# Sorting the routed experts of a two-loop mixture: one sort for the first loop of one group and the second loop of the group ahead of it

## The chip, the cores and the metric

The kernel runs on one NeuronCore of one Trainium2 chip. The metric is device time in microseconds of one execution; a kernel's time is the median of its runs. Lower is better.

## The reference, cut to what matters

A batch of 16 sequences, each 512 tokens by 128 features, goes through four pre-normed residual layers. The last one is what the change is about: a mixture of 8 experts, run twice (two "loops") with the same weights, each token going to its two best experts.

```python
x = x + attn0(layernorm(x))          # 16 heads of 8, no mask
x = x + ffn0(layernorm(x))           # silu-gated, hidden 384
x = x + attn1(layernorm(x))          # 16 heads of 8, q and k normed, causal
x = x + moe(layernorm(x))

def moe(z):
    for _ in range(2):                               # LOOPS
        z_norm = rmsnorm(z, norm_w)
        scores = softmax(z_norm @ router_w)          # 8 experts
        topk_vals, topk_idx = top_k(scores, 2)
        topk_vals = topk_vals / (sum(topk_vals) + EPS)
        mixed = 0
        for e in range(8):
            mixed = mixed + cw[:, e:e+1] * swiglu(z_norm, w1[e], w3[e], w2[e])   # 128 -> 256 -> 128
        z = z + mixed
    return z
```

The second loop of a token depends on nothing but its own first loop, so loops of different sequences may be mixed freely.

## The kernel before

The program is unrolled and every engine's order is fixed by hand. The outer driver is a loop over *slots* (the `while slot < last ...` loop at the end of the kernel), each cut into 7 parts. A sequence takes 32 slots (`PERIOD`) of the first attention (names `s_a`, `e_a`, `mx_a`), starting at slot 32b for sequence b, and 32 slots of the causal second attention (`s_c`, `e_c`, `masked_c`), starting at slot 32b + 73. Each slot issues two exponentials of either stream that is alive; so the n-th `e_a` or `e_c` row of a trace tells which slot it belongs to, and slots can be laid on the time axis. Normally both streams run side by side; from slot 529 on only the causal one is left, and it ends at slot 594.

Between these fixed passes stand *tasks*, generators that are stepped where their pace asks for it: `front(b)` (layer norm, projections, feed-forward), `middle(b)` (the same for the second attention, then `close()`, which finishes the attention layer, writes `zkeep[b]` and `nkeep[b]` to DRAM and routes the sequence for its first loop). `route()` computes the router's logits and writes the one-hot choices (`chosen`) and weights (`cw`) of a sequence; in a trace its matmuls are `pl_m` when `close()` calls it and `pl_r` when the second loop does. The last two sequences (14 and 15) are not sorted: `all_experts` runs every expert on every token (`gg_u`, `gu_u`, `py_u`).

The other 14 sequences form groups, `GROUPS = (3, 3, 3, 3, 2)`. A group is queued (`running`) when its last sequence has been routed, and `experts(grp)` is then the single `active` task. For each of the two loops it does, in order:

- `dispatch`: a counting sort in some twenty small VectorE instructions and two matmuls into `pc`, which gives each (token, choice) a row in a DRAM buffer where every expert's rows are padded to whole tiles of 128. It ends with `owner`, an integer expert number for each tile. Then, for each sequence, one SP load of `znl` from `nkeep` (one buffer) and 8 indirect GpSimd DMAs, the *sends* (`sent<-znl,places`);
- `tiles`: for each tile of 128 rows, in fours: `rows` loaded from `sent` (which waits for all the sends), transposed (`pr`, `rT`), two gate/up and two down passes (`gu`, `h`, `py`, `y`) with that expert's 384 KB of weights, loaded ahead by SP into four buffers `w`; SP reads the expert number from `owner` first (`value_load`). `y` goes back to DRAM (`back<-y`);
- the *gathers*: for each sequence, 8 indirect GpSimd DMAs (`got<-back,places`), and 8 VectorE multiply-adds into `z`. After the first loop the sequence is normed again and routed into the same group; after the second, `xold` is added and the output written.

A sort over n sequences has a fixed number of tiles, `TOP_K * 4 * n + E - 1` = 8n + 7, whatever the data: 31 for n = 3, 23 for n = 2. `pace()` sets how many steps of the active task a slot takes, so that a group is done when the next one is due; no more than two steps go into each of four parts, so 8 a slot. GpSimd and SP keep one order for everything that they do: GpSimd also adds residuals (`x`, `z`), works on the second attention's queries (`both_c`) and raises variances to -0.5 (`rs_*`, `ss_*`).

Of the kernel before, what the change touches and what calls it, by code (L numbers as in the profile page):

```python
# [44 lines left out]
GROUPS = (3, 3, 3, 3, 2)  # L45
# [26 lines left out]
def kernel(  # L72
# [78 lines left out]
    MAXB = max(GROUPS) * NT  # L151
# [235 lines left out]
    groups, x2s = {}, {}  # L387
# [230 lines left out]
    def middle(b):  # L618
# [65 lines left out]
        def close():  # L684
            yield 0
            x2 = x2s.pop(b)
            pool.tensor_tensor(x2, x2, bo_r.unsqueeze(1).to_broadcast([P, NT, D]), ALU.add)
            yield 0
            oT = yield from feature_major(o(), f"o{b}", tag="xT_om", bufs=1)
            po = bank(f"ao_{b}")  # L690
            for k in range(NT):
                pe.matmul(
                    po[:, k * P : (k + 1) * P], oT[:, k * P : (k + 1) * P], w1T[:, 3 * D : 4 * D],
                    start=True, stop=True,
                )
            x3 = xs.tile([P, NT, D], F32, tag="x3", name=f"x3_{b}", bufs=1)
            dve.tensor_tensor(
                x3.rearrange("p t d -> p (t d)"), po, x2.rearrange("p t d -> p (t d)"), ALU.add
            )
            nc.sync.dma_start(xkeep[b], x3)  # L700
            yield 0

            if b >= B - ALL:
                z, mv, rs = yield from layernorm(x3, f"m{b}", tag="qmT_a")
                ss = small.tile([P, NT], F32, tag="ss", name=f"ss_m{b}")
                pool.tensor_tensor(ss, rs, rs, ALU.mult)
                pool.tensor_tensor(ss, ss, mv[:, :, 1], ALU.mult)
                yield 0
                yield from all_experts(b, z, ss)
                return  # L710
            i = next(i for i in range(len(GROUPS)) if b < sum(GROUPS[: i + 1]))
            if i not in groups:
                groups[i] = Group(i)
            z, mv, rs = yield from layernorm(x3, f"m{b}", x3)
            nc.sync.dma_start(zkeep[b], z)
            ss = small.tile([P, NT], F32, tag="ss", name=f"ss_m{b}")
            pool.tensor_tensor(ss, rs, rs, ALU.mult)
            pool.tensor_tensor(ss, ss, mv[:, :, 1], ALU.mult)
            zn = yield from normed(z, ss, f"m{b}_0", z)
            nc.sync.dma_start(nkeep[b], zn)  # L720
            yield from route(zn, groups[i], b - groups[i].first, f"m{b}_0", tag="xT_om", bufs=1)
            if b == sum(GROUPS[: i + 1]) - 1:
                running.append(i)
# [12 lines left out]
    class Group:  # L736


        def __init__(self, i):
            self.i = i  # L740
            self.first = sum(GROUPS[:i])
            self.n = GROUPS[i]
            self.blocks = self.n * NT
            self.tiles = TOP_K * self.blocks + E - 1
            self.loop(0)

        def loop(self, k):
            name = f"{self.i}_{k}"
            nb = self.blocks
            self.chosen = small.tile([P, TOP_K, E, MAXB], F32, tag="chosen", name=f"chosen_{name}")[:, :, :, :nb]  # L750
            self.cw = small.tile([P, TOP_K, MAXB], F32, tag="cw", name=f"cw_{name}", bufs=4)[:, :, :nb]

# [155 lines left out]
    fetched = {loop: [] for loop in range(LOOPS)}  # L908

    def dispatch(grp, loop, dst, name):  # L910
# [34 lines left out]
        picked = small.tile([P, TOP_K, E, MAXB], F32, tag="picked", name=f"picked_{name}", bufs=1)[:, :, :, :nb]  # L945
        for i in range(TOP_K):
            dve.tensor_tensor(picked[:, i], grp.chosen[:, i], upto3, ALU.mult)
# [7 lines left out]
        ends = small.tile([1, MAXT, E], F32, tag="ends", name=f"ends_{name}", bufs=1)[:, :nt]  # L955
# [6 lines left out]
        owner = small.tile([1, MAXT], I32, tag="owner", name=f"owner_{name}")  # L962
        dve.tensor_scalar(owner[:, :nt], ef, float(E - 1), None, ALU.min)
# [3 lines left out]
        for k in range(grp.n):  # L967
            zn = work.tile([P, NT, D], F32, tag="znl", name=f"znl_{name}_{k}", bufs=1)
            nc.sync.dma_start(zn, nkeep[grp.first + k])
            yield FETCH  # L970
            for t in range(NT):
                for i in range(TOP_K):
# [9 lines left out]
                    for load in fetched[loop]:  # L982
                        after(ins, load)
                    grp.sends.append(ins)
                    yield 0
        fetched[loop] = []
        grp.places, grp.owner = places, owner

    def tiles(grp, src, dst, loads, name):

        batches = [(q, min(4, grp.tiles - q)) for q in range(0, grp.tiles, 4)]
# [11 lines left out]
        def fetch(i):  # L1003
            w = work.tile([P, WC], F32, tag="w", name=f"w_{name}_{i}", bufs=4)
            e = nc.sync.value_load(grp.owner[0:1, i : i + 1], min_val=0, max_val=E - 1)
            nc.sync.dma_start(w, wcat[bass.ds(e, 1), :, :].rearrange("e p c -> p (e c)"))
            ws[i] = w

        ws = {}
        for i in range(batches[0][1]):  # L1010
            fetch(i)
        rows = fetch_rows(*batches[0])
        yield FETCH
        for b, (q, n) in enumerate(batches):
# [5 lines left out]
            if b + 1 < len(batches):  # L1020
                rows = fetch_rows(*batches[b + 1])
# [38 lines left out]
    def experts(grp):  # L1060
        for loop in range(LOOPS):
            name = f"{grp.i}_{loop}"
            yield from dispatch(grp, loop, sent[loop], name)
            yield SEND
            yield from tiles(grp, sent[loop], back[loop], fetched[loop], name)
            yield SEND
            places, cw = grp.places, grp.cw
            if loop + 1 < LOOPS:
                grp.loop(loop + 1)
            for k in range(grp.n):  # L1070
                b = grp.first + k
                z = work.tile([P, NT, D], F32, tag="z", name=f"z_{name}_{k}")
                nc.sync.dma_start(z, zkeep[b])
                got = work.tile([P, NT, TOP_K, D], F32, tag="gath", name=f"got_{name}_{k}", bufs=1)
                for t in range(NT):
                    for i in range(TOP_K):
                        j = k * NT + t
                        pool.indirect_dma_start(
                            out=got[:, t, i, :], out_offset=None, in_=back[loop][: grp.tiles * P, :],
                            in_offset=bass.IndirectOffsetOnAxis(ap=places[:, i, j : j + 1], axis=0),  # L1080
                        )
                        yield 0
                yield FETCH
                for t in range(NT):
                    for i in range(TOP_K):
                        j = k * NT + t
                        dve.scalar_tensor_tensor(
                            z[:, t, :], got[:, t, i, :], cw[:, i, j : j + 1], z[:, t, :],
                            ALU.mult, ALU.add,
                        )  # L1090
                    yield 0
                if loop + 1 < LOOPS:
                    nc.sync.dma_start(zkeep[b], z)
                    ss = small.tile([P, NT], F32, tag="ss", name=f"ss_{name}_{k}")
                    sq = work.tile([P, D], F32, tag="y", name=f"zsq_{name}_{k}", bufs=1)
                    for t in range(NT):
                        act.activation(sq, z[:, t, :], AF.Square, accum_out=ss[:, t : t + 1])
                    yield 0
                    pool.tensor_scalar(ss, ss, 1.0 / D, None, ALU.mult)
                    zn = yield from normed(z, ss, f"{name}_{k}")  # L1100
                    nc.sync.dma_start(nkeep[b], zn)
                    yield from route(zn, grp, k, f"r{name}_{k}", tag="xT_r", bufs=1)
                else:
                    xold = work.tile([P, NT, D], F32, tag="znl", name=f"xold_{name}_{k}", bufs=1)
                    nc.sync.dma_start(xold, xkeep[b])
                    yield FETCH
                    pool.tensor_tensor(z, xold, z, ALU.add)
                    nc.sync.dma_start(out[b].rearrange("(t p) d -> p t d", p=P), z)

    def expert_steps(n):  # L1110
        batches = (TOP_K * n * NT + E + 2) // 4
        mixed = n * (TOP_K + 1) * NT
        return LOOPS * (6 + TOP_K * n * NT + 9 * batches + mixed) + 15 * n

    def expert_waits(n):
        return LOOPS * (2 * SEND + (2 * n + 1) * FETCH) + n * FETCH

    def pace(i, now):

        todo, waits = ([count(n) for n in GROUPS[i:]] for count in (expert_steps, expert_waits))  # L1120
        until = PERIOD * (B - 1) + BEHIND + PERIOD + LAG
        rate = sum(todo) / (until - now - sum(waits))
# [48 lines left out]
    while slot < last or tasks or active is not None or running:  # L1171
        slot += 1
        for part in range(NPARTS):
# [5 lines left out]
            if part in PARTS:  # L1179
# [9 lines left out]
                if active is None and running:  # L1189
                    i = running.pop(0)  # L1190
                    grp = groups.pop(i)
# [5 lines left out]
    assert not groups  # L1197
# [31 lines left out]
```

## Time and profile before

| | |
|---|---|
| time of three runs | 3253.62 us (median), 3214.41, 3256.63 |
| the profiled execution | 3232.08 us, its span 3230.4 us |
| mean granted TensorE clock | 0.832 |
| PE (matmul) busy | 2893.9 us, 90% |
| VectorE busy | 2205.2 us, 68% |
| ScalarE busy | 1753.2 us, 54% |
| GpSimd busy | 698.1 us, 22% |
| loads of an expert's weights (`w<-wcat`) | 294, 384 KB each, 4.1 us to landing |
| sends, gathers | 224 and 224, 977 and 976 ns each on GpSimd |
| all DMA | 254.28 MB, 79 GB/s |

Every recorded instruction goes through one helper, so the line number is L59 nearly everywhere and groups are told apart by their tiles. Busy PE is not PE at its peak: matmuls are pipelined and their ends modelled.

### The profile page before, as it was taken

The page shows a single profiled execution, that of the slowest core. Times are in us where ns is not written, and L with a number is a line of the kernel's source. Part 1 is how long each engine was busy: PE and PEld are TensorE (multiplying, and loading weights), DVE is VectorE, ACT ScalarE, POOL GpSimd, SP SyncE. Part 2 cuts the span into 40 slices and gives each one's busy share as a digit, 9 for nine tenths or more (in the row PEclk, how much of TensorE's full clock was granted, in tenths as well). Part 3 has the DMA queues.
Part 4 walks back from the last instruction along what each step waited for, and adds up shares of the span by engine and source line. Part 5 has one row for each costly group of instructions (what it writes and reads, how often), then busy time and mean ns, then how long its engine had stood idle before and what let it go on. Part 6 is the DMA issues. An engine that isn't in the chain of part 4 may idle for free. (4 is left out here: it accounts for less than half of the span.)

```text
span 3230.4 us, 55826 instructions
## 1 busy us (share of the span) xinstructions
PE 2893.9 (90%) x19302; PEld 1732.5 (54%) x19302; DVE 2205.2 (68%) x6700; ACT 1753.2 (54%) x3867; POOL 698.1 (22%) x834
## 2 busy tenths in 40 slices
PE   6999999999998998999989899989989887788978
PEld 3444545455754565565456456446546546465555
DVE  5767677777676768667777866777776664646556
ACT  4656666575654656565566656566655643333322
POOL 1010001003022313303221421330240331412220
PEclk7978878797966998796799889589979859679889
DMA  3000000002411341241133233114224225343441
GB/s 111 4 4 1 8 14 8 14 11 79 137 54 42 109 129 56 87 150 49 50 112 105 77 104 118 43 59 142 83 75 147 90 67 162 97 148 94 131 126 53
DMA packets 192283, 254.28 MB, mean 79 GB/s; under 512 B 18945, under 2 KB 124673, under 8 KB 192001
## 3 DMA queue, kind: packets, MB, share of 16 engines
q1 hardware_dynamic: 176656, 221.16, 22.2%
q0 software_dynamic: 14336, 29.39, 3.2%
q8 instruction: 154, 2.52, 0.3%
q14 instruction: 129, 1.05, 0.1%
q10 hardware_dynamic: 1008, 0.15, 0.0%
HBM read 189.55 MB, written 64.23 MB: 79 GB/s over the span
## 5 line engine op out<-in xcount | busy, mean ns | idle before, releaser
L59 DVE CUSTOM_DVE_ANT_0 masked_c<-s_c,mask 128x128 f32<-128x128 f32 (+3 forms) x1024 | 501.2, 489 | 482.9 <-PE s_c L59 405.0
L59 DVE TENSOR_REDUCE mx_a<-s_a 128x1 f32<-128x512 f32 x1024 | 656.3, 683 | 190.2 <-PE s_a L59 186.9
L59 ACT ACTIVATE e_a<-s_a 128x512 f32<-128x512 f32 x1024 | 556.4, 597 | 245.9 <-PE s_a L59 240.1
L59 ACT ACTIVATE e_c<-s_c 128x512 f32<-128x512 f32 (+3 forms) x1024 | 392.3, 436 | 490.9 <-PE s_c L59 489.6
L59 PE MATMUL s_a<-qkT_a 32*128 32x512 f32 x2048 | 423.5, 576 | 21.6 <-DVE mx_c L59 4.5
L59 PEld LDWEIGHTS s_c<-qkT_c 32*128 32x128 f32 x2048 | 155.8, 215 | 476.6 <-issue 175.9
L59 PE MATMUL s_c<-qkT_c 32*128 32x128 f32 (+3 forms) x2048 | 335.8, 481 | 19.7 <-DVE x L59 6.9
L59 PE MATMUL gu<-rT,w 128*128 128x128 f32 x2352 | 314.5, 284 | 41.4 <-ACT rT L59 18.0
L59 PE MATMUL acc_a<-e_a,vpad 128*32 128x512 f32 x2048 | 351.0, 764 | 0.0
L59 PEld LDWEIGHTS gu<-rT,w 128*128 128x128 f32 x2352 | 285.4, 195 | 73.7 <-ACT rT L59 33.2
L59 POOL DMA_INDIRECT got<-back,places x224 | 218.6, 976 | 295.9 <-DMA back<-y 233.5
L59 PEld LDWEIGHTS s_a<-qkT_a 32*128 32x128 f32 x2048 | 185.9, 210 | 176.8 <-issue 33.3
L59 POOL DMA_INDIRECT sent<-znl,places x224 | 218.8, 977 | 243.7 <-DMA znl<-nkeep 85.2
L59 PE MATMUL s_a<-qmT_a,halves 32*128 32x512 f32 x1024 | 256.4, 494 | 0.0
L59 PE MATMUL acc_c<-e_c,vpad 128*32 128x512 f32 (+3 forms) x2048 | 236.0, 526 | 8.1 <-ACT e_c L59 8.1
L59 ACT ACTIVATE h<-gu 128x256 f32<-128x256 f32 x294 | 112.2, 384 | 170.1 <-PE gu L59 165.3
L59 PE MATMUL py<-w,h 128*128 128x128 f32 x1176 | 164.7, 283 | 9.1 <-DVE h L59 5.6
L59 DVE SCALAR_TENSOR_TENSOR h<-h,gu 128x256 f32<-128x256 f32 x294 | 121.8, 414 | 71.2 <-ACT h L59 70.0
L59 PE MATMUL s_c<-ident_b,mask 128*128 128x128 bf16 x1024 | 164.1, 249 | 0.0
L59 PEld LDWEIGHTS py<-w,h 128*128 128x128 f32 x1176 | 144.9, 192 | 26.8 <-DVE h L59 11.6
L59 PE MATMUL pm_c<-ident_r,mpad 128*128 128x128 f32 x256 | 89.2, 370 | 47.1 <-DVE mpad L59 43.3
L59 DVE TENSOR_TENSOR h<-h,gu 128x256 f32<-128x256 f32 x294 | 123.7, 421 | 10.1
(288 smaller groups left out, 4338.8 us busy)
## 6 DMA issues: line engine op xcount, KB each, us to landing
w<-wcat SPq DMA_DIRECT2D x294, 384.0 KB, 4.1
rows<-sent SPq DMA_DIRECT2D x66, 256.0 KB, 6.4
back<-y SPq DMA_DIRECT2D x66, 256.0 KB, 5.7
w_u<-wcat SPq DMA_DIRECT2D x32, 384.0 KB, 3.2
z<-zkeep SPq DMA_DIRECT2D x28, 256.0 KB, 2.7
znl<-nkeep SPq DMA_DIRECT2D x28, 256.0 KB, 3.0
x<-in_L_attn_x_dram SPq DMA_DIRECT2D x16, 256.0 KB, 3.0
xkeep<-x SPq DMA_DIRECT2D x16, 256.0 KB, 2.0
```

Of the source, the lines that this page charges most:

```text
L59: ins = method(*args, **kwargs)
```

## The change

`GROUPS` becomes seven groups of two. A `Batch` takes the place of a `Group` and holds rows (sequence, loop): batch i sorts the first loop of group i together with the second loop of group i - 1. So there are 8 batches: batch 0 has the first loops of two sequences, batches 1 to 6 have four rows each, batch 7 has the last two second loops. In place of 10 sorts with 8 x 31 + 2 x 23 = 294 tiles there are 8 with 6 x 39 + 2 x 23 = 280.

Batch i is queued as group i was, when its group's last sequence has been routed. Its gathers go first to the first-loop rows, which are normed and routed into batch i + 1 (created then or by the next `close()`, whichever comes first), then to the second-loop rows, which are written out. Batch 7 is queued by batch 6 at its end. The DRAM buffers `sent` and `back` alternate by batch, and grow from 31 to 39 tiles each, which are zeroed at the start.

Three small things go with it: the products of the sort are formed in place in `chosen` (the tile `picked` goes); `ends` takes the buffer of `y`; and `owner` is no longer one instruction in `dispatch` but one for every 16 tiles, made by VectorE just ahead of the weight load of tiles 0, 16 and 32.

```diff
-GROUPS = (3, 3, 3, 3, 2)
+GROUPS = (2, 2, 2, 2, 2, 2, 2)
+OWNERS = 16
...
-    MAXB = max(GROUPS) * NT
+    MAXB = max(a + b for a, b in zip((*GROUPS, 0), (0, *GROUPS))) * NT
...
-    class Group:
+    class Batch:
         def __init__(self, i):
             self.i = i
-            self.first = sum(GROUPS[:i])
-            self.n = GROUPS[i]
+            self.rows = [(b, 0) for b in members(i)] + [(b, 1) for b in members(i - 1)]
+            self.n = len(self.rows)
...
-        picked = small.tile([P, TOP_K, E, MAXB], F32, tag="picked", name=f"picked_{name}", bufs=1)[:, :, :, :nb]
+        picked = grp.chosen
         for i in range(TOP_K):
-            dve.tensor_tensor(picked[:, i], grp.chosen[:, i], upto3, ALU.mult)
+            dve.tensor_tensor(picked[:, i], picked[:, i], upto3, ALU.mult)
...
-        ends = small.tile([1, MAXT, E], F32, tag="ends", name=f"ends_{name}", bufs=1)[:, :nt]
+        ends = work.tile([1, MAXT, E], F32, tag="y", name=f"ends_{name}", bufs=1)[:, :nt]
...
-        owner = small.tile([1, MAXT], I32, tag="owner", name=f"owner_{name}")
-        dve.tensor_scalar(owner[:, :nt], ef, float(E - 1), None, ALU.min)
...
         def fetch(i):
             w = work.tile([P, WC], F32, tag="w", name=f"w_{name}_{i}", bufs=4)
-            e = nc.sync.value_load(grp.owner[0:1, i : i + 1], min_val=0, max_val=E - 1)
+            j = i % OWNERS
+            if j == 0:
+                owner = small.tile([1, OWNERS], I32, tag="owner", name=f"owner_{name}_{i}")
+                n = min(OWNERS, grp.tiles - i)
+                dve.tensor_scalar(owner[:, :n], grp.ends_before[:, i : i + n], float(E - 1), None, ALU.min)
+                owners[i // OWNERS] = owner
+            e = nc.sync.value_load(owners[i // OWNERS][0:1, j : j + 1], min_val=0, max_val=E - 1)
             nc.sync.dma_start(w, wcat[bass.ds(e, 1), :, :].rearrange("e p c -> p (e c)"))
...
     def experts(grp):
-        for loop in range(LOOPS):
-            name = f"{grp.i}_{loop}"
-            yield from dispatch(grp, loop, sent[loop], name)
-            yield SEND
-            yield from tiles(grp, sent[loop], back[loop], fetched[loop], name)
-            yield SEND
-            places, cw = grp.places, grp.cw
+        name, there, here = f"{grp.i}", sent[grp.i % 2], back[grp.i % 2]
+        loads = fetched[grp.i % 2]
+        yield from dispatch(grp, there, loads, name)
+        yield SEND
+        yield from tiles(grp, there, here, loads, name)
+        yield SEND
+        places, cw = grp.places, grp.cw
+        for k, (b, loop) in enumerate(grp.rows):
...
             if loop + 1 < LOOPS:
...
+                then = batch(grp.i + 1)
+                yield from route(zn, then, then.rows.index((b, loop + 1)), f"r{name}_{k}", tag="xT_r", bufs=1)
...
+        if grp.i + 1 == len(GROUPS):
+            running.append(grp.i + 1)
```

## The prediction

> **What bounds the kernel now.** I read the page's busy shares first, then the windows, then GpSimd's timeline and the waits of the last 600 us.
>
> ```profile
> PE 2893.9 (90%) x19302; PEld 1732.5 (54%) x19302; DVE 2205.2 (68%) x6700; ACT 1753.2 (54%) x3867; POOL 698.1 (22%) x834
> PEclk7978878797966998796799889589979859679889
> ```
>
> TensorE is the busiest engine, but 90% and a granted clock that swings between 0.5 and 1 say that a busy microsecond is no fixed amount of work. So I price by windows of 16 slots, cut where a slot's first exponential starts. Columns: start:end, length, busy time (instructions) of PE, PEld, DVE, ACT, POOL, clock, DMA share, GB/s.
>
> ```profile
> 507.70:582.10 74.40, 70.13 (x503) 39.30 (x500) 51.68 (x158) 51.40 (x111) 6.68 (x11) 0.91 0.04 12
> 582.10:651.10 69.00, 65.47 (x412) 32.85 (x404) 50.73 (x159) 40.72 (x86) 6.35 (x6) 0.70 0.03 9
> 651.10:724.20 73.10, 68.97 (x515) 39.54 (x512) 53.39 (x167) 51.82 (x113) 6.68 (x11) 0.95 0.03 12
> 803.50:912.80 109.30, 104.33 (x855) 74.74 (x859) 74.07 (x214) 69.86 (x157) 11.80 (x17) 1.00 0.43 132
> 912.80:1004.50 91.70, 84.75 (x432) 42.89 (x432) 65.98 (x224) 45.18 (x106) 27.93 (x31) 0.56 0.14 41
> 1004.50:1094.10 89.60, 79.65 (x518) 43.32 (x518) 62.80 (x203) 53.53 (x120) 31.84 (x38) 0.81 0.21 65
> 1094.10:1200.80 106.70, 98.07 (x811) 69.76 (x813) 74.96 (x220) 61.65 (x141) 6.34 (x6) 0.98 0.45 137
> 1200.80:1276.30 75.50, 69.90 (x516) 39.85 (x520) 60.58 (x190) 52.00 (x111) 33.70 (x38) 0.95 0.23 63
> ```
>
> The first three (slots 144 to 192) hold no sorted work: mean 72.2 us. The fourth holds 27 tiles, the seventh 31: (109.3 - 72.2)/27 = 1.37 and (106.7 - 72.2)/31 = 1.11, so a tile costs about 1.25 us of time. The fifth holds two second-loop routes and 19 gathers: (91.7 - 72.2)/2 = 9.8 us a route. The sixth holds one route, one sort and 24 sends: 89.6 - 72.2 - 9.8 = 7.6 us a sort. The last holds 24 gathers and nothing else: 3.3 us in all. So in the body sends and gathers are nearly free, and tiles, routes and sorts add up. The tail is different, because one attention stream is gone:
>
> ```profile
> 2679.70:2767.50 87.80, 75.13 (x619) 63.65 (x618) 50.08 (x170) 40.74 (x102) 4.17 (x8) 0.98 0.55 172
> 2767.50:2813.60 46.10, 35.20 (x172) 16.54 (x173) 26.74 (x92) 15.23 (x34) 29.59 (x29) 0.52 0.24 67
> 2813.60:2853.00 39.40, 24.28 (x123) 13.81 (x123) 15.92 (x70) 9.84 (x25) 20.02 (x24) 0.58 0.39 116
> 2853.00:2916.40 63.40, 57.46 (x409) 47.53 (x408) 35.20 (x110) 26.01 (x64) 1.25 (x2) 0.91 0.56 166
> ```
>
> Slots 545 to 558 (second row) hold no tile: 46.1 us, of which TensorE stands 8.9 and 1.7 us, leaves 2.5 us a slot against 4.5 in the body; I use 2.6. In such slots GpSimd is too slow:
>
> ```profile
> 2649.84 1.10 POOL L59 DMA_INDIRECT sent<-znl,places  x1 [3.87 <-DMA znl<-nkeep]
> ...
> 2658.82 0.96 POOL L59 DMA_INDIRECT sent<-znl,places  x1 [0.31 <-issue]
> 2664.66 0.96 POOL L59 DMA_INDIRECT sent<-znl,places  x1 [4.89 <-DMA znl<-nkeep]
> ```
>
> Eight sends take 1.26 us each, and the next sequence's `znl` (one buffer) starts only when they have been read: 14.8 us from one sequence's first send to the next one's. Then the waits between 2660 and 2682 us show who pays, at slot 532:
>
> ```profile
> PE pr L59 <- DMA rows<-sent: 13.5, 1, 13.5
> ```
>
> **The change, part by part.** The slot loop fixes what stands in which slot; I counted it for both kernels from the loop's own rules. Both end at slot 628.
>
> *Slots up to 528.* Tiles 217 before, 218 after: +1.2 us. Sorts 8 before, 6 after: -2 x 7.6 = -15.2. A sort over four rows is wider: from n = 2 to n = 3 the ten VectorE operations whose width grows take 0.73 us more in sum (`placef` 0.373 to 0.484, `go` 0.184 to 0.334, `flat` 0.300 to 0.416 and so on), so I add 0.73 for each of 6: +4.4. Second-loop routes 12 before, 11 after, one having slipped to slot 531: -9.8. Sends and gathers are the same in number and free here. Sum -19.4.
>
> *Slots 528 to 545* (2647.2 to 2767.5 us, 120.3). Before: the second loop of the fourth group, 31 tiles behind a 13.5 us wait for 24 sends. After: no tile and no send, 16 gathers and that route. Price of a tile: first row above, (87.8 - 12 x 2.6)/31 = 1.83 with a `close()` and small waits in it; last row (slots 567 to 572, 23 tiles, four `gg_u` steps at 3.3 of TensorE's busy time), (63.4 - 6 x 2.6 - 13.2)/23 = 1.50. I take 1.65, since a tile's full busy time (gu, py and pr, 314.5 + 164.7 + 47.0 us over 294 tiles) is 1.79. So -31 x 1.65 - 13.5 + 9.8 = -54.9. The gathers: VectorE's `z` stands in order ahead of the attention's maxima, and here a slot is shorter than three gathers; bounds 0 and two waits like the 8.9 us one at slot 550; I take +5. Sum -49.9.
>
> *Slots 545 to the end* (462.9 us). Tiles 46 before, 62 after: 39 in slots 558 to 568 and 23 in 595 to 600; +16 x 1.65 = +26.4, bounds 0 (TensorE has 88 us without a matmul in this stretch) and 1.79 each. Sends: batch 6 emits 32 in slots 547 to 555 and its first `pr` in 557. From first send to `pr` they need 3 x 14.8 + 8 x 1.26 + about 4 for landing and `rows` = 58 us, against ten slots at 2.6: TensorE stands 32 us. Behind them on GpSimd stands `both_c` of sequence 15, for which VectorE, ScalarE and TensorE wait, but within the same 58 us. It takes the place of the waits of 8.9 (slot 550) and 9.5 us (slot 566): +13.6. Batch 7's 16 sends stand between `gg_u` steps, as the last 16 do now: 0. Gathers of batch 6: 32 against 16, +5 as above. Wider sort +0.7. Sum +45.7.
>
> *The owner, every 16 tiles.* SP's `value_load` for tiles 16 and 32 of a batch now waits for a VectorE instruction made just ahead: 2 in each of six batches, 1 in the other two, 14 such waits. Behind it on SP stand the next two weight loads, then `back<-y` and `rows`. VectorE is late by itself (0.17 us) and a maximum (`mx_a`, 0.68): 0.85 us. The weights come ahead by half a four of tiles, some 5 us against 4.1 to landing, and TensorE waits for `w` only 12.9 us in all now. Bounds 0 and 14 x 2 us (a maximum, a masked maximum and two `h` ahead of it: 0.68 + 0.49 + 2 x 0.42); I take a third of 14 x 0.85, +4.
>
> *Free.* `picked` in place, the smaller `ends` buffer (`y` is idle since the batch before), earlier `Batch` tiles: nothing waits. Four more zero DMAs lie in the first 80 us, 500 us before the first send; without that cover, 4 x 3.8 us.
>
> Sum: -19.4 - 49.9 + 45.7 + 4 = -19.6, so 3232.1 - 20 = 3212 for the profiled execution. That one is not the median: the four times known (3214.4, 3232.1, 3253.6, 3256.6) average 3239, and I put the median after at 3239 - 20, about **3220**.
>
> Two rules beside this. The Trainium skill, "Trainium Kernel Development and Optimization", Performance Expectations, calls matmul busy time a bad metric because matmuls are pipelined. The windows agree: 1.79 us busy a tile cost 1.11 to 1.37 in the body; pricing 14 tiles by busy time would give -25 instead of -18. "TensorE: Matmul & The Clock Gate", What's actually happening, says the clock is halved after some 3.4 us of idleness until the engine has been busy as long. The rows agree in kind (0.52 and 0.58 where TensorE stands, 0.98 in tiles); by that rule my 32 us wait, which speaks against the change, would cost some 2 us more as an estimate, and the tile-free slots of 528 to 557 would stay slow.
>
> **The rivals.** *The tail swallows the tiles.* TensorE's 88 empty microseconds after 2767.5 hold all of 16 x 1.79 = 29 and the send chain replaces waits that are there anyway. For: two of three waits in the tail are GpSimd's and fall. Against: in slots 567 to 572 each tile lengthened the slot. Price: 26.4 + 13.6 + 5 fall away: 3239 - 65 = 3174.
>
> *GpSimd becomes the bound of the tail* (the slow side). 32 sends (58 us) and then batch 6's 32 gathers, at about 14 us a sequence with landing and `z`, 56 us, and batch 7's 16 sends, 29 us: 143 in a row, with `both_c`, `x` and `ss` behind them. I have counted 18.6 of it. If nothing of the rest lies beside attention, tiles or `gg_u`, +124: 3343. It is slower by 2% (above 3319) once 118 of the 143 are uncovered. For: waits of TensorE behind GpSimd of 8.3 and 13.4 us at slots 581 and 597 today. Against: `gg_u` slots are 5 to 6 us long and were full in between.
>
> *SP turns out late for owners*: at 2 us each it costs 28 instead of 4: 3244, inside my range.
>
> **How the numbers follow.** Forecast case 0.72 and late owners 0.08, together 0.80, tail swallows 0.12, GpSimd-bound 0.08. Known costs at their best (tiles of the tail free, chain +0) give -65, at worst (owners 28, gathers 9 each, tiles 1.79) about +14; the four executions scatter by 20 around their mean. Range 3176 to 3268. A measurement of this kernel tells about 2% from no change (before's runs span 1.3%); 2% below 3254 is 3189, above it 3319. Faster 0.12, within 0.80, slower 0.08.
>
> **What would show it.** 280 `w` loads; 8 sorts; attention-only stretches of 16 slots still near 72 us, those with 28 tiles near 107. The last stretch with both streams should end some 20 us earlier and slot 545 about 70 us earlier. One TensorE wait of about 30 us on `rows<-sent` near the place of the first 39-tile batch without the first attention, GpSimd busy with 32 sends at 1.26 us before it; `value_load`s that hold no matmul. It is wrong if slot 545 isn't 55 to 80 us earlier, if the tail doesn't grow by 25 to 65, or if TensorE's waits for `w` pass 30 us.

## The result and the profile after

| | before | after |
|---|---|---|
| median of 20 runs | 3231.81 us | 3248.48 us |
| lowest and highest | 3212.94, 3256.63 | 3216.13, 3268.24 |
| the profiled execution | 3232.08 us | 3231.88 us |
| mean granted clock in it | 0.832 | 0.835 |

The ratio after/before is 1.0044, 95% interval [1.0024, 1.0064]: some 14 us slower where the forecast was 20 us faster. The time lies in the forecast range, the sign is wrong, and the two profiled executions are level. So the profiles show what was won and what was given back, and the runs say that slightly more was given back. The ratio leaves out two of the 20 runs after, which were over 1.5% above the fastest; the medians keep them. The profiled execution after is one of the quicker ones, 16.6 us under its kernel's median, while that of before lies at its median: lengths read from the pair flatter the change.

The page of the changed kernel, its busy times, the granted clock in 40 slices and the weight loads:

```profile
PE 2873.1 (89%) x19112; PEld 1714.4 (53%) x19112; DVE 2188.6 (68%) x6650; ACT 1748.9 (54%) x3841; POOL 699.3 (22%) x834
...
PEclk6958977799769978798878979699777976698989
...
w<-wcat SPq DMA_DIRECT2D x280, 384.0 KB, 4.2
```

The work went as announced: 280 loads in place of 294, TensorE 20.8 us less busy, VectorE 16.6 us less, GpSimd as before. The span stayed. The windows of the changed kernel (start:end, length, then busy time and instructions of PE, PEld, DVE, ACT, POOL, granted clock, DMA share, GB/s) say where:

```profile
1274.60:1355.00 80.40, 67.96 (x400) 33.10 (x399) 54.05 (x168) 40.42 (x84) 37.81 (x38) 0.68 0.12 39
1355.00:1468.70 113.70, 109.27 (x869) 77.47 (x868) 75.69 (x219) 71.19 (x158) 6.69 (x11) 0.96 0.47 144
2657.60:2726.80 69.20, 54.88 (x320) 33.11 (x319) 49.77 (x198) 30.86 (x78) 33.52 (x39) 0.73 0.24 69
2726.80:2763.30 36.50, 32.87 (x156) 16.45 (x156) 22.87 (x80) 13.92 (x30) 20.61 (x19) 0.50 0.12 37
2763.30:2901.10 137.80, 89.45 (x681) 75.01 (x680) 50.17 (x157) 42.78 (x107) 19.57 (x23) 0.84 0.54 165
```

The first two rows are 16 slots each of the body: one that holds the sort of a batch of four rows and its 32 sends, one that holds 28 tiles. The prediction priced the sends at nothing; in the first row TensorE stands 12.4 of 80.4 us, against 3.5 to 4.3 us in the prediction's three rows without sorted work. The others are slots 528 to 545, 545 to 557 and 557 to 569. By stages, each cut at the same slot in both profiles:

| slots | before | after | after - before | forecast |
|---|---|---|---|---|
| up to 160 (no sorted work) | 580.6 | 588.6 | +8.0 | 0 |
| 160 to 528 | 2066.6 | 2069.0 | **+2.4** | **-19.4** |
| 528 to 545 | 120.3 | 69.2 | -51.1 | -49.9 |
| 545 to 626 | 453.8 | 494.3 | +40.5 | +45.7 |

The last two stages came out within 6 us. The body did not: 21.8 us are missing. Each length is one execution's, and the clock granted in this stage was 0.833 before and 0.846 after; a profile of nearly the same changed kernel (`owner` made once, below) has 2093.2 us here at 0.827. Steadier is the sum of TensorE's waits between slots 192 and 528: it rose from 152.8 to 174.3 us, and is 171.5 in that other profile. The waits of the whole execution name the candidates (engine and tile that waited, what ended the wait, us in total, times, the longest):

```profile
PE pm_a L60 <- DVE mpad L60: 39.9, 19, 6.6
...
PE gu L60 <- DMA w<-wcat: 32.4, 30, 2.9
...
DVE off_f L60 <- POOL rs_f L60: 31.6, 5, 7.6
...
PE pr L60 <- DMA rows<-sent: 29.9, 1, 29.9
```

Before, the same list of TensorE has 21.0, 12.9 and 16.2 us in the first, second and fourth line, with 2.0, 1.8 and 13.5 us for the longest, and VectorE waits for `rs_f` once, 1.3 us. The fourth line is the wait forecast at slot 557. The first and third are new and belong together. Here is GpSimd's timeline in the changed kernel at one of the five places (start, us, engine, line, operation, tiles, and in brackets the idle time before it and what ended it):

```profile
1336.96 0.99 POOL L60 DMA_INDIRECT sent<-znl,places  x1 [0.17 <-issue]
1343.31 0.96 POOL L60 DMA_INDIRECT sent<-znl,places  x1 [5.36 <-DMA znl<-nkeep]
...
1350.90 0.96 POOL L60 DMA_INDIRECT sent<-znl,places  x1 [0.30 <-issue]
1351.90 0.25 POOL L60 TENSOR_SCALAR rs_f<-mv_f 128x4 f32<-128x4 f32 x1
1352.23 1.04 POOL L60 TENSOR_TENSOR rs_f<-rs_f,mhalf 128x4 f32<-128x4 f32 x1
```

And the waits between 1340 and 1354 us:

```profile
DVE off_f L60 <- POOL rs_f L60: 7.6, 1, 7.6
...
PE pm_a L60 <- DVE mpad L60: 6.6, 1, 6.6
```

GpSimd waits 5.4 us for the one `znl` buffer, then emits seven sends without a pause. Behind them in its order stands `rs_f`, two instructions of 1.3 us in all, the inverse root for the layer norm of some sequence's feed-forward. VectorE stands 7.6 us at `off_f` for it; behind that in VectorE's order stand the maxima of the first attention, so `mpad` is late and TensorE stands 6.6 us in the middle of a slot. The same gap comes once in each of the five batches that have four rows and both attentions beside them, at slots 239, 303, 367, 431 and 495: 3.5, 6.6, 4.9, 3.7 and 5.6 us. The step is 64 slots because a batch now starts every second sequence.

**Theory.** Four rows make a chain of sends of 4 x 14.8 = 59 us (57.3 to 59.2 in the five batches), from the one `znl` buffer and GpSimd's own issue rate; the slots that the loop gives them (my count of its pace) last about 56 us. GpSimd falls behind its own order, and a small operation of another sequence that stands behind sends is late. **Rivals:** the owner, now made during the tiles, delays SP; tiles cost more than 1.25 us when 39 come together; the wait on `rs_f` itself is what costs, whatever the sends do.

### The profile page after: what moved, and what is told of

It reads as the page before. It is cut to its first block, busy times and chain, and to the rows that moved or that the text cites. A ratio compares the mean times of both kernels' runs of the same rounds, so it can differ in the third digit from the quotient of the medians.

```text
span 3230.2 us, 55252 instructions
## 1 busy us (share of the span) xinstructions
PE 2873.1 (89%) x19112; PEld 1714.4 (53%) x19112; DVE 2188.6 (68%) x6650; ACT 1748.9 (54%) x3841; POOL 699.3 (22%) x834
## 4 chain that ended last, share of the span: by engine, by line
PE 59%; DVE 18%; DMA 7%; POOL 6%; issue 6%; ACT 4%; SPq 0%; DVEq 0%; POOLq 0%; ACTq 0%
PE s_a L60 9%; PE acc_a L60 7%; PE s_c L60 7%; PE gu L60 7%; POOL sent L60 5%; DVE masked_c L60 4%; PE acc_c L60 4%; PE py L60 3%; DMA w<-wcat 3%; DVE mx_a L60 3%; PE pm_c L60 2%; PE fg L60 2%; PE fu L60 2%; PE pqk_a L60 2%; PE py_u L60 1%
## 5 line engine op out<-in xcount | busy, mean ns | idle before, releaser
L60 PE MATMUL s_a<-qkT_a 32*128 32x512 f32 x2048 | 430.0, 581 | 15.3 <-DVE h L60 4.1
L60 PE MATMUL gu<-rT,w 128*128 128x128 f32 x2240 | 320.0, 295 | 60.8 <-DMA w<-wcat 32.4
L60 PE MATMUL py<-w,h 128*128 128x128 f32 x1120 | 155.6, 283 | 11.7 <-DVE h L60 9.6
L60 PEld LDWEIGHTS py<-w,h 128*128 128x128 f32 x1120 | 137.3, 193 | 23.1 <-DVE h L60 15.1
L60 POOL TENSOR_TENSOR both_c<-both_c,gains 128x512 f32<-128x512 f32 x16 | 20.3, 1271 | 533.4 <-DVE both_c L60 438.1
```

What stands on the lines that cost most here:

```text
L60: ins = method(*args, **kwargs)
```

## The experiments

Ratios are to runs of the kernel before made beside each experiment (their medians are 3223 to 3231 us), with 95% intervals; the change itself has 1.0044. Stage times and waits are read from one profile each.

### A second `znl` buffer in the changed kernel

```diff
-            zn = work.tile([P, NT, D], F32, tag="znl", name=f"znl_{name}_{k}", bufs=1)
+            zn = work.tile([P, NT, D], F32, tag="znl", name=f"znl_{name}_{k}", bufs=2)
...
-                xold = work.tile([P, NT, D], F32, tag="znl", name=f"xold_{name}_{k}", bufs=1)
+                xold = work.tile([P, NT, D], F32, tag="znl", name=f"xold_{name}_{k}", bufs=2)
```

> The changed kernel with two buffers for znl and xold instead of one, so that a sequence's load no longer waits for the eight sends before it. Theory 1 (GpSimd lags behind its 32 sends, and what stands behind them, the feed-forward's rs_f above all, holds VectorE and then TensorE): a sequence's sends go from 14.8 to about 10.5 us, 32 take some 45 instead of 58; the TensorE gaps of 3.5 to 6.6 us on mpad at slots 239, 303, 367, 431 and 495 (24 us in sum) go, and the wait of 29.9 us on rows in the tail falls to some 15: about 35 us less than the changed kernel, ratio to before near 0.993. Theory 2 (SP late through the owners made every 16 tiles): nothing moves, ratio 1.004. Theory 3 (a fixed phase: in every batch the last four's rT stands on ScalarE behind a cast of the second attention): only the tail's wait shrinks, ratio 1.000.

Measured: **0.9862 [0.98, 0.9925]**, median 3193.23 us. The waits of the whole execution:

```profile
PE pr L60 <- DMA rows<-sent: 16.7, 1, 16.7
...
PE pm_a L60 <- DVE mpad L60: 16.4, 15, 2.0
```

The long waits on `mpad` are gone (longest 2.0 us, as before the change), and the wait for `rows` fell from 29.9 to 16.7. Slots 160 to 528 take 2050.9 us, 18.1 less than in the change at nearly the same clock (0.848 and 0.846). TensorE's waits in slots 192 to 528 are 152.5, those of before. Slots 545 to 626 take 475.0, 19 less than in the change as it was. This version beats both kernels; it gains 1.8% over the change, some 59 us, where I expected 35.

The gain of the body can be placed. In each of the five batches one stretch of 16 slots holds the sort and the 32 sends; here it is at the same place as the first row above (1274.60 to 1355.00):

```profile
1288.00:1361.00 73.00, 67.25 (x397) 32.56 (x396) 53.92 (x168) 39.15 (x82) 37.82 (x38) 0.67 0.14 44
```

It takes 73.0 us in place of 80.4, at a clock of 0.67 and 0.68. The five stretches have a mean of 73.5 us with the second buffer and 79.2 without: 5.7 us a batch, 28.6 in all.

### The owner made once, in `dispatch`, as before

```diff
+        owner = small.tile([1, MAXT], I32, tag="owner", name=f"owner_{name}")
+        dve.tensor_scalar(owner[:, :nt], ef, float(E - 1), None, ALU.min)
...
-            j = i % OWNERS
-            if j == 0:
...
-            e = nc.sync.value_load(owners[i // OWNERS][0:1, j : j + 1], min_val=0, max_val=E - 1)
+            e = nc.sync.value_load(grp.owner[0:1, i : i + 1], min_val=0, max_val=E - 1)
```

> The changed kernel with owner made once in the sort, as before the change. Theory 2: the waits of matmuls on w fall from 32 us back towards 13, some 15 to 20 us less, ratio near 0.999. Theories 1 and 3: no difference from the changed kernel, ratio 1.004, and the waits on w stay, because they lie in the tail's dense tiles, not at tiles 16 and 32.

Measured: 1.0003 [0.9966, 1.004], median 3235.41; the interval overlaps that of the change. Its profile still has `pm_a <- mpad` 39.0 us, `off_f <- rs_f` 32.9 and `pr <- rows` 29.3; only the waits for weights fell, from 32.4 to 24.3. Together with the second buffer:

> Two buffers for znl and owner made once in the sort. If the 0.4% of owner_once is real it adds to that of the second buffer: ratio 0.982. If it was scatter: 0.986.

Measured: 0.9872 [0.9839, 0.9905] against 0.9862 with the buffer alone. Made once, the owner is worth 13 us without the buffer and -3 us with it, so these runs can't tell its cost from 0. As a rival for the body's loss it falls: the waits on `rs_f` stay without the buffer. In both pairs of profiles slots 545 to 626 are shorter with one owner (478.8 and 464.8 us, against 494.3 and 475.0); a cost of some 10 us there isn't excluded.

This pair repeats the test of the buffer, with one owner on both sides and the same clock of 0.827 in slots 160 to 528: 2093.2 us without it and 2067.9 with it, 25.3 less. The five stretches take 80.1 and 74.6 us.

### The feed-forward's root on VectorE, so that nothing waits for `rs_f`

```diff
-        rsqrt(rs, mv[:, :, 1], LN_EPS)
+        if newton:
+            ve = small.tile([P, NT], F32, tag="ve", name=f"ve_{name}", bufs=1)
+            dve.tensor_scalar(ve, mv[:, :, 1], LN_EPS, None, ALU.add)
+            for _ in rsqrt_newton(rs, ve, NT, name, "nwf"):
+                pass
+        else:
+            rsqrt(rs, mv[:, :, 1], LN_EPS)
...
-            xn, _, _ = yield from layernorm(x1, f"f{b}")
+            xn, _, _ = yield from layernorm(x1, f"f{b}", newton=True)
```

> The changed kernel with the reciprocal root of the feed-forward's layer norm made on VectorE (eleven small instructions of Newton's method instead of two of GpSimd), 16 times. Nothing else of the sends changes. Theory 1: the gaps on mpad at the five slots go (24 us), VectorE takes 16 x 2 us more of which little is on TensorE's path: 10 to 20 us less, ratio about 0.999; the wait of 30 us in the tail stays. Theories 2 and 3: the same or a little slower, 1.004 to 1.010.

Measured: 1.0033 [0.9992, 1.0073], median 3247.72. The page:

```profile
PE 2891.7 (89%) x19112; PEld 1721.4 (53%) x19112; DVE 2218.9 (69%) x6842; ACT 1750.3 (54%) x3841; POOL 676.4 (21%) x802
```

`pm_a <- mpad` fell from 39.9 to 19.5 us, none longer than 2.5. But the 12 instructions that each of 16 sequences now has on VectorE brought it from 2188.6 to 2218.9 us, +30.3, and VectorE feeds the same maxima. The run is inconclusive on the price in time: it shows that `rs_f` is what `mpad` waited for, not what that wait was worth. TensorE's waits in slots 192 to 528 did fall by 14.4 us, to 159.9, and the five stretches from 79.2 to a mean of 76.4 (up to three of their sends come just behind them), such as this one:

```profile
1297.80:1372.70 74.90, 67.73 (x401) 33.11 (x400) 56.17 (x182) 40.11 (x84) 33.51 (x33) 0.70 0.13 39
```

### Each sequence's sends one slot later

```diff
             nc.sync.dma_start(zn, nkeep[b])
-            yield FETCH
+            yield FETCH + 1.0
```

> The changed kernel with one slot more of waiting after each load of znl, before its eight sends are issued, so that GpSimd can keep up (about 4.1 slots a sequence against 3.1). Theory 1: in the body the five gaps on mpad shrink or go (10 to 24 us), in the tail the chain of sends is GpSimd's own and stays at 58 us: ratio about 1.000. Theory 2: 1.004. Theory 3: the tile stage moves by four slots, and the 3.2 us waits of the last four's rT (16 us in five batches) move or go with it whatever GpSimd does.

Measured: 0.9932 [0.99, 0.9965], median 3212.47. Giving GpSimd more slots for the same sends makes the kernel *faster*: slots 160 to 528 take 2046.5 us, 22.5 less than in the change, though at a clock of 0.856, the highest of these profiles; TensorE's waits in slots 192 to 528 are 154.8, and `off_f <- rs_f` falls from 31.6 to 10.5. I had expected a ratio of about 1.000. Slots 528 to 545 take 14.9 us longer and the stage after them 23.8 less, which I hadn't foreseen. The sends' number is the same, so it isn't the number alone that costs.

### Half the sends, in both kernels

```diff
                 for i in range(TOP_K):
+                    if i:
+                        yield 0
+                        continue
                     j = k * NT + t
```

> The changed kernel without the sends of every token's second choice (16 instead of 32 a batch; the tiles then work on stale rows, all steps stand in the same slots). It takes away half of GpSimd's chain and nothing else. Theory 1: four sequences take 4 x (4 x 1.26 + 4.8) = 39 us instead of 58, GpSimd doesn't lag in the body (about 28 us less) and the tail's wait of 30 us shrinks to about 11: ratio 0.989 to 0.992. Rival (the body's loss is a fixed phase of tiles against the attention steps): only the tail's 19 us, ratio 0.9985.

> The kernel before without the sends of every token's second choice, as the control. Theory 1: its chains of 24 (44 us) and 16 hardly lag in the body, so only the tail's waits of 13.5 and 9.5 us shrink: ratio 0.993 to 0.997. Rival (fewer sends are worth the same in either kernel): ratio 0.985 to 0.988.

Measured: 0.9825 [0.9794, 0.9855] with the change, 0.9926 [0.9895, 0.9957] without. The same 112 sends fewer are worth 2.2% of 3232 us (71 us) after the change and 0.7% (24 us) before it. In slots 160 to 528 the edit saves 3.9 us before the change (2066.6 to 2062.7) and 16.5 after it (2069.0 to 2052.5). TensorE's waits in slots 192 to 528 say it more clearly: 152.8 and 153.8 us before the change, 174.3 and 144.2 after it. So "sends are free in the body" was right for the kernel that I read it from and wrong for the one that I applied it to. With half the sends in both, the change brings 10.2 us in this stage. The waits of the halved, changed kernel:

```profile
PE pm_a L60 <- DVE mpad L60: 17.2, 16, 2.0
...
PE pr L60 <- DMA rows<-sent: 11.1, 1, 11.1
```

Again the long waits on `mpad` are gone, this time without a new buffer and without touching `rs_f`. Three ways of loosening the chain (a buffer, more slots, fewer sends) give the body 16.5 to 22.5 us back, and a fourth that leaves the chain and removes only `rs_f` takes 14.4 us of waits away but shows no gain in time. The rival that only the wait on `rs_f` matters isn't excluded, since its run paid with VectorE's time. Nor is the chain's length separated from what stands behind it. From a sort's first send to its last, half the sends take 34 to 38 us in place of 40 to 44 in the first six sorts before the change, and 44 to 50 in place of 56 to 58 in the five batches after it. So GpSimd lags in either kernel, and before the change that lag cost next to nothing. The edit saved more than I expected of it; 32 of the 56 us by which the two changed profiles differ lie behind slot 545, 18.8 of them in the wait for `rows`.

### The second buffer in the kernel before

> The kernel before with two buffers for znl and xold. Theory 1 (the changed kernel's 32 sends are a chain longer than the slots given to it, 24 are not): the body stays, only the waits on rows at slots 532 (13.5 us) and 566 (9.5 us) shrink, some 12 us: ratio 0.996. Rival (two buffers help any kernel of this kind as much, so that the chain isn't what the change lost): the same 1.8% as for the changed kernel, ratio 0.982.

Measured: 1.0079 [1.0048, 1.0109], median 3256.93: the same edit that gains 1.8% after the change loses 0.8% before it. Waits between 1632 and 1646 us:

```profile
DVE off_c L59 <- POOL rs_c L59: 9.5, 1, 9.5
...
PE s_a L59 <- DVE mx_c L59: 8.4, 1, 8.4
```

The buffer lets the hand-written order place sends closer together. In the kernel before, `rs_c`, the root for the second attention's norm, stood behind 15 of a sort's 24 sends at this place; now it stands behind 23, and TensorE waits 3.4, 8.4, 9.4 and 7.9 us at slots 252, 348, 444 and 528. It is the mechanism of the change with another victim. My expectation priced the buffer by the wait for `znl` that it removes and forgot what it moves.

### Buffer and slow sends together

> Two buffers for znl and one slot more of waiting ahead of each sequence's sends. Theory 1: both take the same lag away, so the second adds little in the body: ratio 0.982 to 0.988. If their gains have separate causes they add up: 0.975.

Measured: 1.0000 [0.9975, 1.0026]; two edits that gain 1.8% and 1.1% over the change gain 0.4% together. GpSimd's timeline at one of the new gaps, and the waits there (2105 to 2117 us):

```profile
2107.04 0.96 POOL L60 DMA_INDIRECT sent<-znl,places  x1 [0.30 <-issue]
2112.76 0.96 POOL L60 DMA_INDIRECT sent<-znl,places  x1 [4.76 <-DMA znl<-nkeep]
2113.74 1.27 POOL L60 TENSOR_TENSOR x<-x,o_a 128x512 f32<-128x512 f32 x1
```

```profile
DVE st_f L60 <- POOL x L60: 8.7, 1, 8.7
...
PE s_c L60 <- DVE mx_a L60: 8.3, 1, 8.3
```

Now it is `x`, the residual ahead of the feed-forward's norm, that stands one send behind a wait for `znl`. TensorE loses 6.1, 8.3 and 7.9 us at slots 365, 429 and 493, again 64 slots apart, while in the tail the wait for `rows` is down to 6.5. Which small operation lies behind a burst decides, and each edit draws that anew.

### Batches that start four slots later

```diff
-                if active is None and running:
+                if active is None and running and ready is None:
+                    ready = now + (4.0 if running[0] < 6 else 0.0)
+                if active is None and running and now >= ready:
+                    ready = None
```

> The changed kernel with batches 0 to 5 started four slots later than they are queued; 6 and 7 as they are. Theory 1: the chain of sends is as long, but the feed-forward's rs_f now meets it in its third sequence, where GpSimd lags less, so the gaps on mpad shrink and others (rs_a, rs_m) may come: ratio 0.998 to 1.004. Theory 3 (phase against ScalarE): the 16 us of waits on the last four's rT go, whatever GpSimd does: ratio 0.999.

Measured: 1.0105 [1.0057, 1.0153]. Moving the phase by four slots did not take `rs_f` out of the way; the same five gaps grew to 5.8 to 8.1 us, and `pm_a <- mpad` to 54.6 in all. TensorE's wait of the last four tiles of a batch for `rT`, 3.2 us each in the change, went away, and `py <- h` rose from 9.6 to 28.6 us. As a cure it failed; as a probe, the gaps and the time grew together.

### The prices of a tile and of a sort

Four empty tiles more in each of eight batches, in the changed kernel:

```diff
-            self.tiles = TOP_K * self.blocks + E - 1
+            self.tiles = TOP_K * self.blocks + E - 1 + 4
```

> The changed kernel with four empty tiles more at the end of every batch (8 x 4 = 32; their rows are read by nobody). It measures the price of a tile: by the prediction's 1.25 us in the body and 1.65 in the tail 24 x 1.25 + 8 x 1.65 = 43 us, 1.3% over the changed kernel, ratio 1.018. If a tile costs its whole busy time of 1.79 us, 57 us, ratio 1.022; if tiles are half hidden, ratio 1.010.

Measured: 1.0233 [1.017, 1.0295]; over the change 1.9% or 61 us, 1.9 us a tile, with some 0.6 to either side. It is above my 1.25 of the body and 1.65 of the tail, but not beyond them with certainty.

The kernel before with the groups of two alone, 14 sorts and 322 tiles:

```diff
-GROUPS = (3, 3, 3, 3, 2)
+GROUPS = (2, 2, 2, 2, 2, 2, 2)
```

> The kernel before with seven groups of two, loops sorted apart: 14 sorts of 23 tiles, 322 tiles. It shows what the merging alone takes away. By the prediction's prices 28 tiles more at 1.25 us and 4 sorts more at 7.6 make +65 us, ratio 1.020; sends come 16 at a time, so theory 1 adds nothing. If tiles and sorts are really worth half of what I read, ratio 1.010.

Measured: 1.0228 [1.0163, 1.0293], 73 us, with some 21 to either side, where the prices of tiles and sorts gave 65. So their sum is not far off in this kernel, though the run tests neither price alone, and sorting the two loops together does save what smaller groups cost. What is missing in the change is a term that was set to nothing.

## Why the prediction was wrong

**Slots up to 528: -19.4 forecast, +2.4 measured. This step failed,** and in it the sentence "Sends and gathers are the same in number and free here". Their number was the same; their grouping was not. I read the price from windows of three-row groups. Four rows in one chain last 57 to 59 us, and in each of five batches one small operation came to lie behind seven sends: 24.3 us of gaps in TensorE. A second buffer takes 18.1 and 25.3 us out of the body, in two pairs at like clocks, and 28.6 and 27.1 us out of the five stretches with the sends. So the term that was put at 0 was worth some 18 to 29 us. Whether the rest of the sum (+1.2, -15.2, +4.4, -9.8) came out isn't shown: with the buffer the body is 15.7 us shorter than before in one profile (clock 0.848) and 1.3 us longer in the other (0.827).

The price also had no row of its own. Only gathers had one; the row with 24 sends (1004.50 to 1094.10) was charged to its route and its sort. And that row was the longest of its kind. The same 16 slots of the next two groups, with the same route, sort and 24 sends:

```profile
1558.70:1643.50 84.80, 74.64 (x516) 40.63 (x514) 62.46 (x203) 53.40 (x119) 31.84 (x38) 0.87 0.20 62
2104.70:2189.60 84.90, 74.88 (x518) 40.93 (x513) 62.40 (x203) 53.36 (x120) 31.86 (x38) 0.87 0.22 69
```

By the prediction's own working they leave 2.8 and 2.9 us for a sort and its sends, not 7.6. After the change a sort with 32 sends costs 79.2 - 72.2 = 7.0 us on average, with the second buffer 1.3. So by these rows the term of -15.2 us for two sorts fewer was too large, and a sort became dearer with its longer burst.

The prediction had the tool in hand: it worked out the 14.8 us chain for the tail, and named `both_c` behind it there, but did not put the same chain against the body's slots.

**Slots 528 to 545: -49.9 forecast, -51.1 measured.** Right.

**Slots 545 to the end: +45.7 forecast, +40.5 measured**, within the stated 25 to 65. The one wait on `rows` was put at 32 us and came to 29.9, in the slot named. (Two readings behind it were a little off: the wait put at 8.9 us at slot 550 is 8.1 in TensorE's list, and 46.1 us less the two waits is 2.7 us a slot over 13 slots, not 2.5; I used 2.6.) The rival in which empty time swallows the tiles is out, and so is the one in which GpSimd binds the whole tail. But the same rival's idea, small operations behind sends in GpSimd's order, was true 300 slots earlier.

**The owner: +4 forecast;** not to be told from 0 with two pairs of runs (13 us and -3 us). TensorE's waits for `w` passed the 30 us that I had named as a sign of being wrong (32.4), but only 8 us of that went away with the owners; what the rest comes from, and whether it costs anything, isn't settled.

**The signs.** 280 loads, 8 sorts, the long wait and the tail's growth are there; the 28 tile stretch took 113.7 against "near 107". Slot 545 came 40.7 us earlier against 55 to 80, and the last stretch with both streams ended 10 us later in place of 20 earlier. By its own criterion the forecast is wrong, and in the body.

**The total.** With the body put at what the pair of profiles shows, the sum of -19.6 becomes +2. The pair says -0.2, of which +8.0 arose before slot 160, where no sorted work stands; that stretch takes 569 to 598 us in the profiles of the changed kernel and its variants, so it is scatter. The ratio says +14 and the medians +17. The dozen microseconds between are about what the profiled execution lies under its kernel's median (16.6); in which stage the typical run loses them these profiles don't show.

**The pages.** The rule of the Trainium skill that speaks for this cure, "Trainium Kernel Development and Optimization", Best Practices, advises double buffering for performance, to overlap DMA with compute. The runs agree for one kernel (0.9862) and disagree for the other (1.0079), so the measurement decides: here the buffer's worth went with what it did to GpSimd's order.

## What to carry to other kernels

Price an engine that keeps one order by its longest burst against the time of the slots that the burst is given, and list the small operations of other streams that stand behind it; GpSimd was busy 22% of the span and still set the sign of this change. A price read from one grouping ("free here") holds for that burst length only. When the period of a burst changes (96 to 64 slots here), look again at what lies behind it; and a buffer that is added is also a new order, so run it in each kernel before calling it a gain.

## What the runs showed of the hardware

- One program on one core scatters with its granted clock: in the 20 runs of the changed kernel the mean clock is 0.823 to 0.845, the time 3216 to 3268 us, with a correlation of -0.93 and some 22 us for each 0.01 of clock. A single pair of profiles could not have shown the 14 us.
- The clock can stay at half while TensorE seems busy. Two windows of slots 545 to 557 in the changed kernel (columns as above):

```profile
2738.00:2748.00 10.00, 9.52 (x41) 3.77 (x37) 7.38 (x25) 3.83 (x8) 6.99 (x7) 0.50 0.15 48
2758.00:2764.00 6.00, 5.96 (x28) 2.65 (x26) 2.44 (x11) 3.00 (x7) 2.77 (x3) 0.50 0.19 52
```

TensorE is shown busy 95% and 99% of the time, for 10 and 6 us, at a clock of 0.50. The Trainium skill, "TensorE: Matmul & The Clock Gate", What's actually happening, has the full clock return after a busy window of some 3.4 us. These rows differ, at least where busy is what the profile calls busy: 41 matmuls in 10 us, with modelled ends. Whether the gate counts another kind of activity no run here shows.
